# Attention layer 1 in hand-ordered steps: grouping of tiled matmuls, split transposes, value copies on ScalarE, range checks inside the loop

## The chip, the cores and the metric

One core of one Trainium2 chip. The metric is the device time of one execution in microseconds (us); lower is better. Each run is classed as fast or slow by its time and granted clock. A ratio is the mean time of one kernel's fast runs over that of the other's of the same rounds, so not quite the ratio of the medians quoted beside it. "Faster" means by more than 2%.

The engines are called as in the profile: PE (TensorE), PEld (its weight loads), DVE (VectorE), ACT (ScalarE), POOL (GpSimd), SP (SyncE, which issues the DMAs here).

## The reference, cut to what matters

Two layers run over x of 128 x 256 x 256 (rows, positions, channels). Only the second is touched: group norm, then attention within a band of 16 positions, four heads of 64 channels, for each of the 128 rows.

```python
def _L1_conv_ref(x, w_in, b_in, w_out, b_out, band):
    qkv = x2 @ w_in.T + b_in                      # x2: rows x 256 x 256
    q, k, v = jnp.split(qkv, 3, axis=-1)          # four heads of 64 each
    scores = jnp.einsum('bhid,bhjd->bhij', q, k) / jnp.sqrt(D)
    scores = jnp.where(jnp.abs(i - j) <= band, scores, -jnp.inf)
    attn = jax.nn.softmax(scores, axis=-1)
    out = jnp.einsum('bhij,bhjd->bhid', attn, v)
    return out @ w_out.T + b_out
...
x = x + _L1_conv_ref(_gn(x), L1_conv_w_in, ..., 16)
```

Softmax weights of a position sum to 1. A bias of the values therefore comes through attention unchanged, and can be added after it, as `b_v @ w_out.T`.

## The kernel before

Layer 1 handles two rows (a pair) at a time, 64 pairs. A generator prepares the next pair step by step while the present one is scored and applied; the framework's scheduler then fixes the final order on each engine. The names in the profile: `ps_x` transposes, `ps_p` projections of q and k, `ps_v` values, `ps_sc` scores, `ps_o` and `ps_su` the two parts of apply (outputs and sums), `ps_y` the output projection. PE's results lie in banks of PSUM until ACT or DVE have copied them out (an evacuation). `ps_mm` has two PSUM banks, which transposes, projections, values and outputs take in turn. Scores and apply work on tiles of 64 rows (tiled groups); all other groups use the full array of 128 x 128. The lists of the profile show two instructions for each fp32 matmul of the program: a projection of two matmuls is x4.

```python
def prep1(p, d):                                   # next pair, in steps
    xt = sb.tile([P, 2 * NB, C], F32, name="xt1", tag="xt", bufs=3)
    nc.sync.dma_start(xt, rows(x1[s0 // GB], s0 % GB, 2))
    ...
    nc.gpsimd.tensor_tensor(xb, xt, bcast(bout_r, 1, 2 * NB), ALU.add)
    ...
    for k in range(KC):                            # all eight transposes
        ps = mm1("ps_x1")
        for t in range(2 * NB):
            nc.tensor.transpose(ps[...], xt[:, t, k * P : (k + 1) * P], ident)
        nc.scalar.activation(xgT[:, k, :], ps, AF.Identity, bias=nM1[:, k : k + 1])
    yield
    ...                                            # q0 q1 k0 k1, a yield after each
    for r in range(2):                             # values, with their bias on VectorE
        ...
        nc.vector.tensor_tensor(v[:, r, :, :], ps.rearrange(...), bcast(bv1_r, 1, NB), ALU.add)
        yield
...
for p in range(NP):
    for r in range(2):
        es = scores1(d, r)                         # 64x64 tiles, exp, band mask
        next(ahead, None); next(ahead, None)
        late = bool(ends1)
        if todo1: back1()                          # apply (64x32 tiles) and combine
        next(ahead, None)
        if late: end_row1()                        # output projection, sum, store
        next(ahead, None)
        todo1.append((d, r, es))
...
# after the loop: range checks of eb (4096 columns), both sums (2048, 1024), mask (256)
check(eb.rearrange("p h b i -> p (h b i)"), math.exp(-20.0), math.exp(20.0), 0, ck)
...
def check(src, lo, hi, col, pool):
    ...
    nc.vector.tensor_scalar(a, src, lo, None, ALU.is_gt)
    nc.vector.scalar_tensor_tensor(a, src, hi, a, ALU.is_lt, ALU.mult)
    nc.vector.tensor_reduce(ok[:n, col : col + 1], a, AX.X, ALU.min)
```

## Time and profile before

| | before |
|---|---|
| time, median of 4 fast runs | 3526.7 us (3524.7 to 3528.1) |
| first transposes of layer 1 to last output add | 1303.8 us |
| one pair of rows | 20.27 us |
| last output add to end of span | 32.3 us |

The lines behind the table stand in the prediction. How to read them: in a timeline each line is a merged group with its start, duration, engine, source line, operation, names and count. Matmuls overlap in the pipeline, so durations of neighbouring groups overlap too. What a group costs PE is the distance from its start to the start of the next group.

### The profile page before, as it was taken

How to read it: one execution, taken by the hardware profiler on the slowest of the kernel's cores; microseconds unless marked ns; L12 is line 12 of the kernel's file. 1: busy time of each engine (PE TensorE's matmuls, PEld its weight loads, DVE VectorE, ACT ScalarE, POOL GpSimd, SP SyncE). 2: the span in 40 equal slices, each digit the busy share in tenths (PEclk: the TensorE clock that was granted, in tenths of full speed). 3: DMA queues.
4: the chain of work that ended last, by engine and by line, in shares of the span. 5: the costliest groups of instructions: out<-in, count | busy, mean ns of one | idle time of the engine just before them, and what ended most of it. 6: DMA issues, size and time to landing. Idle time of an engine off the chain costs nothing.

```text
span 3522.3 us, 80789 instructions
## 1 busy us (share of the span) xinstructions
PE 3315.2 (94%) x35154; PEld 2034.1 (58%) x35154; DVE 2035.7 (58%) x3284; ACT 1373.5 (39%) x1937; POOL 1975.4 (56%) x1385
## 2 busy tenths in 40 slices
PE   5666999999999999999999996999999999999995
PEld 3333555555555555555555554666666666666664
DVE  5863566666666666666666664444444444444445
ACT  2332444444444444444444442333333333333331
POOL 2356877777777877777777774223323323323331
PEclk8787999999999999999999998999999999999998
DMA  9961122212221222122212221111111111112111
GB/s 285 322 188 45 47 70 70 71 46 70 70 70 46 70 70 71 46 70 70 71 50 76 71 63 60 50 50 62 50 50 62 50 50 62 50 51 61 50 48 48
DMA packets 246812, 263.13 MB, mean 75 GB/s; under 512 B 46000, under 2 KB 212912, under 8 KB 246320
## 3 DMA queue, kind: packets, MB, share of 16 engines
q1 hardware_dynamic: 246448, 257.88, 25.0%
q8 instruction: 278, 4.55, 0.6%
q14 instruction: 86, 0.70, 0.1%
HBM read 189.02 MB, written 68.81 MB: 73 GB/s over the span
## 4 chain that ended last, share of the span: by engine, by line
PE 88%; DMA 3%; ACT 3%; DVE 2%; SPq 2%; POOL 2%; issue 0%; ACTq 0%; DVEq 0%; POOLq 0%
PE ps_p L1233 20%; PE ps_p L1546 14%; PE ps_sc L1267 8%; PE ps_ov L1298 7%; PE ps_v L1560 7%; PE ps_v L1248 6%; PE ps_y L1340 6%; PE ps_y L1630 6%; PE ps_su L1304 3%; PE ps_sc L1585 3%; PE ps_o L1612 3%; DMA zt<-in_z_dram 2%; PE ps_x L1215 2%; ACT e L1593 1%; PE ps_su L1612 1%; ACT xgT L1538 1%
## 5 line engine op out<-in xcount | busy, mean ns | idle before, releaser
L1288 POOL TENSOR_TENSOR eboth<-e 128x512 f32<-128x512 f32 x512 | 640.2, 1271 | 401.4 <-DVE e L1283 401.3
L1283 DVE TENSOR_TENSOR e<-ps_sc,eb 128x1024 f32<-128x1024 f32 x512 | 603.0, 1219 | 338.7 <-ACT ps_sc L1274 249.1
L1274 ACT ACTIVATE ps_sc<-ps_sc 128x1024 f32<-128x1024 f32 x512 | 492.8, 1006 | 507.4 <-PE ps_sc L1267 507.4
L1595 POOL TENSOR_TENSOR e<-e,bw 128x384 f32<-128x384 f32 x256 | 251.2, 1003 | 475.5 <-ACT e L1593 475.5
L1546 PE MATMUL ps_p<-xgT,w_in 128*128 128x512 f32 x1024 | 500.7, 612 | 4.2
L1531 POOL TENSOR_TENSOR xb<-xt,bout_r 128x1024 f32<-128x1024 f32 x64 | 150.7, 2356 | 423.5 <-DVE yo L1634 418.8
L1267 PE MATMUL ps_sc<-qT,kT 32*128 32x256 f32 x4096 | 293.8, 400 | 1.6 <-ACT kT L1237 1.6
L1564 DVE TENSOR_TENSOR v<-ps_v,bv_r 128x512 f32<-128x512 f32 x128 | 84.4, 660 | 362.6 <-PE ps_v L1560 362.6
L1621 DVE TENSOR_TENSOR odd<-ps_o,odd 128x512 f32<-128x512 f32 x128 | 88.5, 692 | 339.9 <-ACT odd L1618 339.8
L1233 PE MATMUL ps_p<-xnT,wq 128*128 128x512 f32 x512 | 255.7, 622 | 20.5 <-POOL xnT L1221 20.5
L1298 PE MATMUL ps_ov<-e,v 128*32 128x256 f32 x4096 | 274.1, 385 | 0.5 <-DVE oT L1312 0.5
L1546 PEld LDWEIGHTS ps_p<-xgT,w_in 128*128 128x128 f32 x1024 | 179.0, 189 | 163.0 <-issue 106.7
L1233 PE MATMUL ps_p<-xgT,wg 128*128 128x512 f32 x512 | 253.9, 618 | 0.0
L1340 PE MATMUL ps_y<-wo,oT 128*128 128x256 f32 x1024 | 243.9, 381 | 7.1 <-POOL oT L1330 7.1
L1560 PE MATMUL ps_v<-w_in,xgT 128*128 128x256 f32 x1024 | 248.3, 385 | 0.0
L1340 PEld LDWEIGHTS ps_y<-wo,oT 128*128 128x128 f32 x1024 | 195.6, 191 | 88.1 <-issue 59.5
L1630 PE MATMUL ps_y<-w_out,oT 128*128 128x256 f32 x1024 | 243.5, 381 | 3.0 <-DVE oT L1623 3.0
L1248 PE MATMUL ps_v<-wv,xnT 128*128 128x256 f32 x1024 | 242.1, 379 | 0.0
L1233 PE MATMUL ps_p<-xnT,wk 128*128 128x512 f32 x512 | 241.9, 595 | 0.0
L1267 PEld LDWEIGHTS ps_sc<-qT,kT 32*128 32x128 f32 x4096 | 185.4, 184 | 94.2 <-issue 70.5
L1630 PEld LDWEIGHTS ps_y<-w_out,oT 128*128 128x128 f32 x1024 | 194.9, 191 | 56.9 <-issue 31.9
L1620 DVE RECIPROCAL rv<-odd 128x256 f32<-128x256 f32 x128 | 224.4, 1753 | 4.3
(159 smaller groups left out, 5090.1 us busy)
## 6 DMA issues: line engine op xcount, KB each, us to landing
xa<-in_x_dram SPq DMA_DIRECT2D x8, 4096.0 KB
xt<-in_x_dram SPq DMA_DIRECT2D x64, 512.0 KB
rvb<-rsum SPq DMA_DIRECT2D x256, 128.0 KB
x<-xo SPq DMA_DIRECT2D x16, 2048.0 KB
xt<-x SPq DMA_DIRECT2D x64, 512.0 KB
out_dram<-yo SPq DMA_DIRECT2D x64, 512.0 KB
rs_r<-rs_d SPq DMA_DIRECT2D x64, 256.0 KB
rs_d<-lrs SPq DMA_DIRECT2D x64, 2.0 KB
```

Source lines behind the costliest of these rows:

```text
L1233: nc.tensor.matmul(ps, w[:, k, m * P : (m + 1) * P], getattr(self, src)[:, k, :], start=(k == 0), stop=(k == KC - 1),)
L1248: nc.tensor.matmul(self.ps_v[:, b * C : (b + 1) * C], self.xnT[:, k, t * P : (t + 1) * P], wv[:, k, :], start=(k == 0), stop=(k == KC - 1),)
L1267: nc.tensor.matmul(self.pss[q // 2][:, q % 2, b, :], self.kT[rs, c, r * I + b * P : r * I + (b + 1) * P], self.qT[rs, c, r * I : (r + 1) * I],
L1274: nc.scalar.activation(self.pss[a], self.pss[a], AF.Exp)
L1283: nc.vector.tensor_tensor(e, pss[a], eb[:, h : h + 2], ALU.mult)
L1288: nc.gpsimd.tensor_tensor(t, es[a][:, :, 0, :], es[a][:, :, 1, :], ALU.add)
L1298: nc.tensor.matmul(ov[q * D0 : (q + 1) * D0, :], self.v[:, r, b, h * D0 : (h + 1) * D0], es[q // 2][:, q % 2, b, :], start=(b == 0), stop= ...
L1340: nc.tensor.matmul(self.ps_y[:, b * C : (b + 1) * C], self.oT[r][:, k, b * P : (b + 1) * P], wo[:, k, :], start=(k == 0), stop=(k == KC - 1),)
L1546: nc.tensor.matmul(ps, w_in[:, k, n * C + m * P : n * C + (m + 1) * P], xgT[:, k, :], start=(k == 0), stop=(k == KC - 1),)
L1560: nc.tensor.matmul(ps[:, b * C : (b + 1) * C], xgT[:, k, t * P : (t + 1) * P], w_in[:, k, 2 * C : 3 * C], start=(k == 0), stop=(k == KC - 1),)
L1595: nc.gpsimd.tensor_tensor(e[:, q], e[:, q], bcast(bw.rearrange("p b w -> p (b w)"), 1, KC), ALU.mult)
L1630: nc.tensor.matmul(ps[:, b * C : (b + 1) * C], oT[:, k, b * P : (b + 1) * P], w_out[:, k, :], start=(k == 0), stop=(k == KC - 1),)
```

## The change

It takes the order of layer 1 out of the scheduler's hands. Scores of one row are followed straight by apply of the row before; the transposes of a pair are split over both steps; values are copied by ScalarE without bias, which moves into the output's bias; and the range checks are cut to 512 columns and run one in an iteration. The output's bias is added to the input in place, after its transposes. In the last pair two value groups are moved between the rest, and each row is stored by itself; the sums of the last eight pairs are checked without a way through memory. In the loop `was`, `now`, `nxt` and `nn` are the pair before, the present one and the next two; `turn` transposes, `combine` adds and divides the parts of apply, `out_row` is output projection, sum and store.

```diff
-    bv1_r = load_row(b_in[2 * C : 3 * C], "bv1_r")
+    bv_c = const.tile([P, KC], F32, name="bv_c")          # four small loads
...
+        for k in range(KC):
+            nc.tensor.matmul(ps[:, :C], bv_w[:, k, :], w_out[:, k, :], ...)
+        nc.vector.tensor_add(bout_r, bout_r, ps[:, :C])   # value bias, through w_out
...
+                self.xt = sb.tile(..., tag="xt", bufs=4)
+            def turn(self, k):                            # four transposes, not eight
+                ...
+                if k == KC - 1:
+                    nc.gpsimd.tensor_tensor(self.xt, self.xt, bcast(bout_r, 1, 2 * NB), ALU.add)
...
-                nc.vector.tensor_tensor(v[:, r, :, :], ps..., bcast(bv1_r, 1, NB), ALU.add)
+                nc.scalar.copy(self.v[:, r, :, :].rearrange("p b c -> p (b c)"), ps)
...
+        with tc.manual_schedule():
+            for p in range(NP - 1):
+                nn = pair1(p + 2)                         # issues the load
+                ...
+                now.scores(0)
+                was.apply(1)
+                was.out_row(0)
+                was.combine(1)
+                nxt.project("qT", 0)
+                nxt.project("kT", 0)
+                nxt.project("qT", 1)
+                nn.turn(0)
+
+                now.scores(1)
+                now.apply(0)
+                now.combine(0)
+                nxt.project("kT", 1)
+                if p < NP - 2:
+                    nxt.values(0)
+                    nxt.values(1)
+                was.out_row(1)
+                nn.turn(1)
+                if checks and p > 0:
+                    checks.pop(0)()
+                was, now, nxt = now, nxt, nn
...                                                       # last pair written out
```

## The prediction

> **What bounds the kernel now.** I read the page first (engine shares, the slices), then busy time by windows, then TensorE's timeline of one pair of rows in layer 1, then VectorE's timeline at the end. Page and windows:
>
> ```profile
> PE 3315.2 (94%) x35154; PEld 2034.1 (58%) x35154; DVE 2035.7 (58%) x3284; ACT 1373.5 (39%) x1937; POOL 1975.4 (56%) x1385
> PE   5666999999999999999999996999999999999995
> 2186.20:3489.30 1303.10, 1295.56 (x19968) 862.02 (x19968) 592.77 (x767) 464.47 (x768) 399.32 (x320) 1.00 0.17 53
> 2351.98:2372.25 20.27, 20.20 (x314) 13.45 (x313) 9.28 (x12) 7.25 (x12) 6.23 (x5) 1.00 0.17 54
> 3490.00:3522.30 32.30, 0.56 (x2) 0.50 (x2) 21.56 (x15) 0.00 (x0) 0.00 (x0) 0.55 0.20 72
> ```
>
> The columns of the windows are PE, weight loads, DVE, ACT, POOL, granted clock, DMA share and GB/s. Layer 1, which is all that changes but for setup, runs from 2186.2 to 3489.3: 64 pairs, one every 20.27 us. PE is busy in 99% of it, at full clock; the next engine, DVE, in 46%. So a change in layer 1 pays only if it shortens PE's own sequence. The last 32.3 us are another stage: PE idle, DVE busy alone. What fills a pair on PE (start, duration, group):
>
> ```profile
> 2351.98 0.93 PE L1612 MATMUL ps_o<-e,v 64*32 64x96 f32 x60
> ...
> 2353.27 1.99 PE L1560 MATMUL ps_v<-w_in,xgT 128*128 128x256 f32 x8
> 2355.11 1.89 PE L1630 MATMUL ps_y<-w_out,oT 128*128 128x256 f32 x8
> 2356.93 0.89 PE L1585 MATMUL ps_sc<-qT,kT 64*64 64x96 f32 x32
> 2357.75 1.15 PE L1537 MATMUL ps_x<-ident,xt 128*128 128x128 f32 x8
> 2358.82 0.51 PE L1612 MATMUL ps_o<-e,v 64*32 64x96 f32 x18
> 2359.41 1.98 PE L1546 MATMUL ps_p<-xgT,w_in 128*128 128x512 f32 x4
> 2361.32 0.73 PE L1612 MATMUL ps_o<-e,v 64*32 64x96 f32 x40
> ...
> 2362.43 1.98 PE L1546 MATMUL ps_p<-xgT,w_in 128*128 128x512 f32 x4
> 2364.25 1.89 PE L1630 MATMUL ps_y<-w_out,oT 128*128 128x256 f32 x8
> 2365.98 1.88 PE L1546 MATMUL ps_p<-xgT,w_in 128*128 128x512 f32 x4
> 2367.79 0.89 PE L1585 MATMUL ps_sc<-qT,kT 64*64 64x96 f32 x32
> 2368.61 1.98 PE L1546 MATMUL ps_p<-xgT,w_in 128*128 128x512 f32 x4
> 2370.43 1.89 PE L1560 MATMUL ps_v<-w_in,xgT 128*128 128x256 f32 x8
> 2372.25 0.93 PE L1612 MATMUL ps_o<-e,v 64*32 64x96 f32 x60
> ```
>
> Read starts, not durations (those overlap). The same four projection instructions take 1.82 from start to next start at 2368.61, which follows a tiled group (64-row tiles); 1.81 at 2365.98, which precedes one; 1.91 at 2359.41, which does both. The y group takes 1.73 at 2364.25, with a full-array group on both sides, and 1.82 at 2355.11, before a tiled one. So going into a tiled stretch costs 0.09 us and coming out 0.10, **about 0.20 us an excursion**, and a projection without either is 1.72. There are five excursions a pair: apply; scores; the first 18 instructions of the other apply; its other 78; scores. That second apply also costs 0.58+1.11 = 1.69 in two pieces, against 1.29 for the whole one.
>
> The end of the run:
>
> ```profile
> 3493.09 2.29 DVE L946 TENSOR_SCALAR chk<-eb 128x4096 f32<-128x4096 f32 x1 [3.06 <-DMA out_dram<-yo]
> 3495.42 4.43 DVE L947 SCALAR_TENSOR_TENSOR chk<-eb,chk 128x4096 f32<-128x4096 f32 x1
> ...
> 3515.58 0.15 DVE L1697 TENSOR_SCALAR verdict<-ok_ps 1x1 int32<-1x1 f32 x1 [0.69 <-PE ok_ps L1696]
> ```
>
> The last output is added at 3490.03, the checks run alone until 3514.7, and the verdict stands at 3515.73, 6.6 us before the end of the span.
>
> **What the Trainium skill says.** "TensorEngine Tiling (Array Packing)", Key Properties: changing the tiling mode drains TensorE. The trace agrees in kind: 0.20 us for each excursion. "Perfetto Trace Analysis", Identifying the Most-Contended Engine: matmul busy time does not tell how close PE is to its limit. It agrees: 20.20 of 20.27 us count as busy with all those switches inside. "TensorE: Matmul & The Clock Gate", Back-to-back issue gap, has 262 cycles for 256 columns and 518 for 512; at the 2.4 GHz named there that is 0.11 and 0.22 us. This trace steps 0.216 and 0.43 in fp32, twice as much, and I use the trace. The same page, The HAM clock gate, has the array at half clock after an idle window; the first transposes of layer 1 step 0.214 us instead of 0.109 after such a pause, so both ends of the loop run partly slow, before and after.
>
> **The change, part by part.**
>
> *PE order.* The instruction order of the changed kernel has per pair: scores, apply, y, three projections, four transposes; then scores, apply, one projection, two values, y, four transposes. Counts of real work stay. Scores and apply now adjoin, so there are two excursions, and apply is never split. Working: 4 projections x 1.72 = 6.88; 4 value and y groups x 1.73 = 6.92; 2 scores x 0.82 = 1.64; 2 applies x 1.29 = 2.58; 8 transposes x 0.109 = 0.87; sum 18.89; 2 x 0.20 = 0.40; **19.29 us a pair**. Checked on the kernel before: the same 18.89 + 5 x 0.20 + 0.40 for the split = 20.29, measured 20.27. That scores followed straight by apply costs no more than 0.82 is seen in the last pair before, at 3471.59 to 3472.41. Gain 0.97 us a pair; one pair's worth is left out for the first and last, so 63 x 0.97 = **61 us**.
>
> *Range checks.* They go into the loop in pieces of 512 columns, by the rows of the old checks about 0.4+0.7+0.7 = 1.8 us of DVE in some 15 of the iterations; DVE is over half idle there. At the end, between the last output add and the verdict, 0.16+0.07+0.56+0.2 = 1.0 us remain, then the 6.6 us: 7.6 in place of 32.3, so **24.7 us** less. The last row's own check (1.1 us at 256 columns) lies in front of the last output add, where DVE had waited 3.4 us for PE.
>
> *Values by ScalarE.* 2 x 0.66 us a pair leave DVE, 2 x 0.59 (the copy of the same shape) come to ACT: 8.4 of 19.3 us there. Off the path: 0. The bias goes through w_out once (two matmuls and an add before the loop): under 1 us.
>
> *Ends.* The final drain keeps its stalls (apply waiting for the combine before it, y waiting for the last combine: 0.3+0.9+1.9 us before), with two value groups moved there to fill some. The first pair is as serial as it was. Net 0, give or take 3.
>
> Sum: 61 + 24.7 = 86 us; 3527.9 - 86 = **3442 us**, -2.4%.
>
> **Rivals.** (a) *The fixed order makes PE wait.* The load of a pair two ahead is now issued at the top of an iteration, after the previous output, and its transposes come after scores, apply, y and three projections: some 8 us later. One load issued at 2340.38 had its last packets at 2343.9, beside an output: 3.5 us. Against it, then; were the load as slow as 9 us, 1 us a pair would come back, 3505 us. The accumulators are the other place: the second apply needs the combine of the first, which on DVE stands behind the y add: 1.83 (y) + 0.25 + 0.68 + 0.41 + 1.75 + 0.69 = 5.6 us after that apply, and PE comes there after 8.3. Slack 2.7 us. (b) *Switches are not what costs*, and each weight change costs the same wherever it is: then only the split of apply (0.40) goes, 25 + 25 = 50 us, 3478. Against: 1.73 and 1.82 for the same y group, by its neighbour alone. (c) *The clock.* PE denser by 5% might be granted less; the loop has 1.00 now. A grant of 0.97 gives back about 37 us: 3479. Nothing speaks for it. (d) *ACT or DVE become the bound*: 8.4 and under 10 of 19.3 us; only their order could hurt, by late release of the two projection banks; each evacuation (0.69 us) has a 1.7 us group beside it.
>
> **Range and chances.** The end stage is nearly sure. The loop is my risk: 0.1 us a pair is 6 us. 0.25 us more than I worked out, from semaphores at the short transposes or an unforeseen wait, would bring 3458, just the 2% line (3457). Fewer switch costs than thought, or a shorter start, could give 10 us more. I take 3428 to 3464. Faster by over 2%: 0.79; within 2%: 0.20; slower: 0.01.
>
> **What would show it.** In the changed profile: a pair every 19.3 us (19.1 to 19.5); scores to apply 0.82 apart with no other group between; no apply in two pieces; projections of 1.72 inside a run of three; no PE wait of over 0.15 us in the loop; checks of 512 columns between the adds and under 9 us from the last output add to the end. A period of 19.8 or more with a wait before the first transposes or before the second apply would make rival (a) right; a period of 19.8 with no waits, rival (b); a granted clock under 0.99 in the loop, (c).

## The result, and the profile after

3439.7 us (median of 4 fast runs, 3437.7 to 3441.4) against 3526.7; ratio 0.9754, 95% interval 0.9737 to 0.9771. Faster by 2.5%; 3442 was predicted.

The windows of the changed kernel: layer 1, one pair, and what follows the last output add. The columns are as in the prediction.

```profile
2186.10:3429.47 1243.37, 1238.83 (x19970) 874.75 (x19970) 598.56 (x714) 545.84 (x896) 407.82 (x320) 1.00 0.19 57
2816.33:2835.60 19.27, 19.27 (x317) 13.66 (x313) 8.11 (x10) 8.53 (x14) 6.24 (x6) 1.00 0.19 56
3429.47:3435.90 6.43, 0.00 (x0) 0.00 (x0) 0.05 (x2) 0.00 (x0) 0.00 (x0) 0.50 0.20 64
```

Layer 1 starts at the same time in both profiles (2186.2 and 2186.1). From there to the last output add it is 60.5 us shorter (1303.83 - 1243.37); from there to the end, 32.3 - 6.5 = 25.8 us. Together 86.3 of the 86.4 us between the spans. PE was busy 99.4% of this stage before and is busy 99.6% of it now, at full clock both times, and the profile notes no wait of PE (over 0.15 us) from 2250 to 3400 us in either kernel: the busy share does not show the gain, the number of pairs per time does. PE's timeline of a pair shows where it lies:

```profile
2814.22 0.89 PE L1605 MATMUL ps_sc<-qT,kT 64*64 64x96 f32 x32
2815.04 0.93 PE L1633 MATMUL ps_o<-e,v 64*32 64x96 f32 x60
...
2816.33 1.99 PE L1664 MATMUL ps_y<-w_out,oT 128*128 128x256 f32 x8
2818.16 5.31 PE L1576 MATMUL ps_p<-xgT,w_in 128*128 128x512 f32 x12
2823.31 0.60 PE L1565 MATMUL ps_x<-ident,xt 128*128 128x128 f32 x4
2823.84 0.89 PE L1605 MATMUL ps_sc<-qT,kT 64*64 64x96 f32 x32
2824.66 0.93 PE L1633 MATMUL ps_o<-e,v 64*32 64x96 f32 x60
...
2825.95 1.98 PE L1576 MATMUL ps_p<-xgT,w_in 128*128 128x512 f32 x4
2827.78 3.62 PE L1591 MATMUL ps_v<-w_in,xgT 128*128 128x256 f32 x16
2831.23 1.89 PE L1664 MATMUL ps_y<-w_out,oT 128*128 128x256 f32 x8
...
2833.49 0.89 PE L1605 MATMUL ps_sc<-qT,kT 64*64 64x96 f32 x32
```

From 2814.22 to 2833.49 is one pair, 19.27 us. There are two stretches of tiled groups (64-row tiles): scores and whole apply, 0.82 + 1.29 us each. The three projections in a row cost 5.15, or 1.72 each. No line carries a wait. The end, on DVE:

```profile
3428.78 0.69 DVE L1668 TENSOR_TENSOR yo<-ps_y,xt 128x512 f32<-128x512 f32 x1 [0.78 <-PE ps_y L1664]
3429.39 0.13 DVE L1760 TENSOR_SCALAR verdict<-ok_ps 1x1 int32<-1x1 f32 x1
```

The verdict follows the last add at once; all that remains is a tail of 6.4 us, which the kernel before has too (6.6).

### The profile page after: what moved, and what is told of

It reads as the page before.

```text
span 3435.9 us, 81082 instructions
## 1 busy us (share of the span) xinstructions
PE 3257.9 (95%) x35158; PEld 2048.2 (60%) x35158; DVE 2019.8 (59%) x3218; ACT 1455.3 (42%) x2065; POOL 1982.7 (58%) x1385
## 5 line engine op out<-in xcount | busy, mean ns | idle before, releaser
L1615 POOL TENSOR_TENSOR e<-e,bw 128x384 f32<-128x384 f32 x256 | 258.9, 1033 | 444.1 <-ACT e L1613 444.1
L1576 PE MATMUL ps_p<-xgT,w_in 128*128 128x512 f32 x1024 | 469.4, 601 | 0.1
L1568 POOL TENSOR_TENSOR xt<-xt,bout_r 128x1024 f32<-128x1024 f32 x64 | 151.9, 2374 | 383.9 <-PE ps_x L1565 383.9
L1668 DVE TENSOR_TENSOR yo<-ps_y,xt 128x512 f32<-128x512 f32 x128 | 88.3, 690 | 379.1 <-PE ps_y L1664 379.1
L1576 PEld LDWEIGHTS ps_p<-xgT,w_in 128*128 128x128 f32 x1024 | 188.9, 190 | 199.8 <-issue 166.6
L1591 PE MATMUL ps_v<-w_in,xgT 128*128 128x256 f32 x1024 | 231.8, 379 | 0.0
L1591 PEld LDWEIGHTS ps_v<-w_in,xgT 128*128 128x128 f32 x1024 | 194.4, 190 | 53.5 <-issue 30.1
L1255 PEld LDWEIGHTS ps_v<-wv,xnT 128*128 128x128 f32 x1024 | 189.6, 190 | 50.9 <-issue 31.1
```

The lines of the kernel that those rows point to most:

```text
L1255: nc.tensor.matmul(self.ps_v[:, b * C : (b + 1) * C], self.xnT[:, k, t * P : (t + 1) * P], wv[:, k, :], start=(k == 0), stop=(k == KC - 1),)
L1576: nc.tensor.matmul(ps, w_in[:, k, n * C + m * P : n * C + (m + 1) * P], self.xgT[:, k, :], start=(k == 0), stop=(k == KC - 1),)
L1591: nc.tensor.matmul(ps[:, b * C : (b + 1) * C], self.xgT[:, k, t * P : (t + 1) * P], w_in[:, k, 2 * C : 3 * C], start=(k == 0), stop=(k == ...
L1615: nc.gpsimd.tensor_tensor(e[:, q], e[:, q], bcast(bw.rearrange("p b w -> p (b w)"), 1, KC), ALU.mult)
```

## The experiments

Theory: in the loop PE waits for nothing, and only its own order counts; each excursion from full-array matmuls to tiled ones and back costs 0.20 us, and cutting apply costs more; the rest of the gain is the bare checks at the end. Rivals: hand order as such (fewer waits), the move of work to other engines, or only the uncut apply.

Start times of layer 1 differ by up to 11 us between runs and chips before anything that was changed. So beside the times I give the length of a pair and the stage from the first transposes of layer 1 to the last output add, both from the traces. That stage was 1243.4 in the changed kernel's own profile, and 1242.1 in two variants with the same loop (e5, e6): differences of 2 us are nothing. Most of that comes from the first projections, during which the granted clock comes back from 0.50 to 1.00, sooner or later: they take 8.95 us to the next group in the changed kernel's profile, 7.99 in e5 and 7.78 in e6, whose start is the same. Without them the three stages agree within 0.4 us.

| kernel | median us (before, same chip) | ratio, 95% interval | pair us | stage us | end us |
|---|---|---|---|---|---|
| before | 3526.7 | | 20.27 | 1303.8 | 32.3 |
| changed | 3439.7 (3526.7) | 0.9754 (0.9737 to 0.9771) | 19.27 | 1243.4 | 6.5 |
| e1, group between | 3469.9 (3531.3) | 0.9824 (0.9807 to 0.9840) | 19.67 | 1266.9 | 6.8 |
| e4, apply cut | 3470.9 (3531.3) | 0.9829 (0.9813 to 0.9845) | 19.73 | 1269.7 | 6.9 |
| e2, old order, late load | 3928.9 (3531.3) | 1.1124 (1.1105 to 1.1142) | 27.29 | 1727.0 | 6.9 |
| e3, the same, cut | 3933.6 (3531.3) | 1.1137 (1.1118 to 1.1156) | 27.30 | 1730.9 | 6.8 |
| e9, old order | 3462.2 (3526.6) | 0.9817 (0.9802 to 0.9832) | 19.62 | 1264.3 | 7.0 |
| e10, old order, cut | 3503.2 (3526.6) | 0.9932 (0.9917 to 0.9947) | 20.27 | 1305.4 | 6.9 |
| e8, transposes together | 3475.3 (3527.0) | 0.9855 (0.9838 to 0.9871) | 19.83 | 1277.8 | 6.5 |
| e5, checks last | 3467.1 (3527.0) | 0.9831 (0.9815 to 0.9847) | 19.27 | 1242.1 | 34.7 |
| e6, no checks | 3439.5 (3527.0) | 0.9753 (0.9737 to 0.9769) | 19.27 | 1242.1 | 6.5 |
| e7, values on VectorE | 3444.1 (3527.0) | 0.9765 (0.9749 to 0.9782) | 19.27 | 1246.4 | 6.9 |
| e11, ends mended | 3439.5 (3526.6) | 0.9753 (0.9740 to 0.9767) | 19.27 | 1241.6 | 6.5 |

All gave correct results.

### e1: one full-array group between scores and apply

```diff
                 now.scores(0)
-                was.apply(1)
                 was.out_row(0)
+                was.apply(1)
...
                 now.scores(1)
-                now.apply(0)
-                now.combine(0)
                 nxt.project("kT", 1)
+                now.apply(0)
+                now.combine(0)
```

> The changed kernel with one full-array group put between scores and apply in both steps (the y group in the first, the fourth projection in the second). Same instructions, two more excursions between tiled and full-array matmuls per pair. Theory (mode switches cost 0.20 us each): a pair takes 19.27 + 2 x 0.197 = 19.66 us, the whole +25 us against the changed kernel, about 3465 us, and the scores are followed by a y group at the same 0.82 us. Rival (what counts is that the order is by hand and apply is whole, not who stands beside whom): 19.27 us, 3440 us.

Measured: 19.67 us a pair, +0.40; the stage 23.5 us longer. PE's timeline:

```profile
2806.69 0.89 PE L1605 MATMUL ps_sc<-qT,kT 64*64 64x96 f32 x32
2807.51 1.98 PE L1576 MATMUL ps_p<-xgT,w_in 128*128 128x512 f32 x4
2809.42 0.93 PE L1633 MATMUL ps_o<-e,v 64*32 64x96 f32 x60
```

The scores still cost 0.82. The projection between two tiled groups costs 1.91, with no wait noted, where it cost 1.82 after apply and 1.72 in a run. Same instructions, same dependencies met; only the neighbours changed. This shows the price of a switch, and refutes the rival that hand order itself, whatever it is, gives the gain. What in the array takes the time is not shown. The trace gives one hint: inside a run of full-array groups the weight load begins a step ahead of its matmul (in the changed kernel at 2827.35 for the value matmul of 2827.78), but after a tiled group it begins with its matmul (both at 2825.95).

### e4: apply cut, and nothing else

```diff
-                was.apply(1)
-                was.out_row(0)
+                was.apply(1, 0, 9)        # its first nine products: 18 instructions
+                was.out_row(0)
+                was.apply(1, 9, 48)
```

> The changed kernel with only the first apply cut after 18 instructions by the y group. Theory: one more excursion and the cut, +0.46 us a pair: 19.73 us, +29 us, about 3469 us. Rival (only the excursion counts, the cut itself is free): +0.20, 19.47 us, +12 us, 3452 us.

Measured: 19.73 us, +0.46, as expected. PE's timeline:

```profile
2814.39 0.52 PE L1637 MATMUL ps_o<-e,v 64*32 64x96 f32 x18
2814.84 1.99 PE L1668 MATMUL ps_y<-w_out,oT 128*128 128x256 f32 x8
2816.76 0.73 PE L1637 MATMUL ps_o<-e,v 64*32 64x96 f32 x40
...
2817.87 5.42 PE L1576 MATMUL ps_p<-xgT,w_in 128*128 128x512 f32 x12
```

The two pieces take 0.45 + 1.11 = 1.56 us in place of 1.29: 0.26 (before rounding) is the cut itself. The excursion is the other 0.20, seen in the y group (1.92 for 1.83) and the projections behind the second piece. How the 0.26 divides between a second end and a second start, no run separates.

### e2 and e3: the old order by hand, with a slip of mine

In these two I moved the eight transposes to the place they had before (right after the first scores), but let them be those of the pair two ahead, whose load is issued at the top of the same iteration.

```diff
                 now.scores(0)
+                nn.turn(0)
+                nn.turn(1)
                 was.apply(1)
-                was.out_row(0)
                 was.combine(1)
                 nxt.project("qT", 0)
+                nxt.project("qT", 1)
+                was.out_row(0)
                 nxt.project("kT", 0)
-                nxt.project("qT", 1)
-                nn.turn(0)

                 now.scores(1)
-                now.apply(0)
-                now.combine(0)
                 nxt.project("kT", 1)
                 ...
                     nxt.values(0)
+                now.apply(0)
+                now.combine(0)
                 ...
                     nxt.values(1)
                 was.out_row(1)
-                nn.turn(1)
```

In e3 the first apply is also cut: `was.apply(1, 0, 9)`, then `nxt.project("qT", 0)`, then `was.apply(1, 9, 48)`.

> The order of groups of the kernel before, laid down by hand in the changed kernel, apply left whole. Theory: four excursions instead of two, in place of 2 x 0.20 some 0.79 us, so 18.89 + 0.8 = 19.7 us a pair, +27 us, about 3466 us. Rival (hand order as such removes waits): near 19.3 us a pair, 3440 us.

> As the run with the old order, with the first apply cut after 18 instructions by a projection, as it stood in the kernel before. Theory: a fifth excursion (0.20) and the cut itself (0.17 for the second end of a tiled group, 0.09 for its second start), +0.46 over that run: about 20.15 us a pair, +55 us over the changed kernel, about 3494 us; the remaining 0.1 to the 20.27 of the kernel before is its projection's wait for the transposed input, which this order does not have. Rival: the cut costs only where it waits, so no more than the run with the old order.

Both missed by far: 27.3 us a pair. SP's timeline of e2 (the issue of a load), then PE's:

```profile
2817.94 0.46 SPq L1557 DMA_DIRECT2D xt<-x  x1
```

```profile
2822.99 1.94 PE L1565 MATMUL ps_x<-ident,xt 128*128 128x128 f32 x8 [5.61 <-DMA xt<-x]
2824.86 1.53 PE L1633 MATMUL ps_o<-e,v 64*32 64x96 f32 x64
```

PE stands for the load in every pair, 5.3 us on average (37 waits, the longest 5.6), and then works at half clock for a while (granted 0.50 from 2822.99 to 2827; eight transposes take 1.87 us to the next group, 1.02 in e9). They tell nothing of the switches, but they are the test that rival (a) of the prediction needed. The load can be used 5.05 us after its issue here, the slowest of 33 (4.6 to 5.05, median 4.8), with an output store of the same size issued 0.5 us ahead of it. The prediction had read 3.5 us off the packets of a load whose store was 2.4 us ahead. In the changed kernel the issue is at 2815.07 and the transposes at 2823.31, 8.24 us later. So the order does hold, with some 3.2 us to spare and not the 4.5 I had counted. A step moved carelessly costs 7.7 us a pair (27.29 against 19.62 in e9), where the whole gain of the loop is 1.00.

### e9 and e10: the old order, its load in time

The same order with `nxt.turn(0)` and `nxt.turn(1)` in place of `nn.turn`, so that a load is a whole pair ahead, as in the kernel before; e9 with apply whole, e10 with it cut where the scheduler had cut it.

```diff
-        for k in range(KC):               # before the loop
-            nxt.turn(k)
...
                 now.scores(0)
-                nn.turn(0)                # against e2; e10: the same against e3
-                nn.turn(1)
+                nxt.turn(0)
+                nxt.turn(1)
```

> The order of the kernel before by hand once more, now faithfully: the transposes are those of the pair projected in the same iteration, so their input was loaded a whole pair earlier. In the first try the transposes came 0.8 us after the issue of their load and TensorE waited 5.6 us for it in every pair, which hid everything else. Apply whole. Theory (0.20 us an excursion): four excursions, 19.7 us a pair, +27 us over the changed kernel, about 3467 us. Rival (hand order as such is the gain): 19.3 us, 3440 us.

> The same with the first apply cut after 18 instructions by the first projection, which is the very order of the kernel before. Theory (the order on TensorE is the whole difference in the loop): the cut and the fifth excursion bring +0.46, the projection's wait for its transposed input some 0.1 more: 20.27 us a pair as before, +63 us over the changed kernel, about 3502 us. Rival (other parts of the change, such as the in-place sum or the values by ScalarE, carry some of the gain): clearly under 20.2 us.

Measured: 19.62 and 20.27 us a pair. PE's timeline of e10:

```profile
2806.55 0.89 PE L1605 MATMUL ps_sc<-qT,kT 64*64 64x96 f32 x32
...
2808.39 0.51 PE L1637 MATMUL ps_o<-e,v 64*32 64x96 f32 x18
2809.03 1.98 PE L1576 MATMUL ps_p<-xgT,w_in 128*128 128x512 f32 x4
2810.94 0.73 PE L1637 MATMUL ps_o<-e,v 64*32 64x96 f32 x40
...
2826.82 0.89 PE L1605 MATMUL ps_sc<-qT,kT 64*64 64x96 f32 x32
```

With the old order of groups the changed kernel has the old length of a pair, to 0.01 us, though values are still on ScalarE, the sum still in place, the checks still inside and the order still by hand. So **the order of the groups on PE is the whole gain of the loop**. From the changed kernel to e9 it is 0.35 for two excursions, not 0.40: with only the eight transposes between scores and apply, the excursion costs 0.15 (1.02 us against 8 x 0.109 = 0.87). From e9 to e10 it is 0.65: 0.20 the excursion, 0.26 the cut (as in e4), and 0.19 that the first piece of apply takes 0.64 us to the next start where 0.45 was its own: the projection behind it waits for the transposed input, which the trace names ACT `xgT`. (From the end of the scores to that projection it is 1.66 us in e10 and in the kernel before alike, though the pieces between divide it differently.) e10 as a whole is 23.4 us under the kernel before by medians: the end of the program, which it kept.

### e8: the transposes together

```diff
                 nn.turn(0)
+                nn.turn(1)
...
                 was.out_row(1)
-                nn.turn(1)
```

> The changed kernel with both groups of transposes at the end of the first step. Theory (two banks): the second group takes the bank of the projection just before the first one, which ScalarE frees about 0.95 us after that projection ends, while the first transposes take 0.44: a wait of 0.5 us a pair, 19.8 us, +31 us, about 3471 us. Rival (the split does not matter; number of excursions is the same): 19.27 us, 3440 us.

Measured: 19.83 us, +0.56; the stage +34.4. PE's timeline:

```profile
2822.14 0.60 PE L1565 MATMUL ps_x<-ident,xt 128*128 128x128 f32 x4
2823.08 0.66 PE L1565 MATMUL ps_x<-ident,xt 128*128 128x128 f32 x4 [0.34 <-ACT qT L1580]
```

The second four start 0.94 us after the first, where 0.44 is their work: they want the bank of the projection just before the first four, and `qT` is the evacuation of that bank. Four transposes are too short to cover an evacuation of 0.69 us; with a long group behind each of them, as in the split, nothing waits. So in this order the transposes are better split, though that saves no switch.

### e5 and e6: the checks after the loop, and no checks

```diff
-                if checks and p > 0:
-                    checks.pop(0)()
...
+        while checks:                     # e5; e6 drops them
+            checks.pop(0)()
         tot = sm.tile([P, 1], F32, name="okmin", bufs=1)
```

> The changed kernel with its fifteen range checks of 512 columns (1.8 us each on VectorE by the changed kernel's trace: 0.42 + 0.69 + 0.69) put after the loop. Theory: they lie bare at the end, 15 x 1.8 = +27 us, about 3467 us, and the pair stays at 19.27 us. Rival (the checks in the loop cost something there, so taking them out gives part back): less than +20 us and a shorter pair.

> The changed kernel without the fifteen checks (those of the last pairs stay), so not a kernel to use. Theory: VectorE has the time, so nothing changes in the loop: 3440 us, within 2 us. Rival: VectorE's checks hold up an evacuation now and then, and the time falls by up to 15 x 0.5 = 7 us.

e5: +27.4 us by medians, all in the end (34.7 against 6.5), the pair unchanged. Its window after the last add shows DVE busy alone:

```profile
3430.53:3465.20 34.67, 0.56 (x2) 0.50 (x2) 25.88 (x47) 0.00 (x0) 0.00 (x0) 0.50 0.03 10
```

e6 (which omits part of the guard, so is no kernel to use) is as long as the changed kernel: 3439.5 against 3439.7. Inside the loop the checks cost nothing that can be measured.

### e7: the values on VectorE, with their bias

```diff
-                nc.scalar.copy(self.v[:, r, :, :].rearrange("p b c -> p (b c)"), ps)
+                nc.vector.tensor_tensor(self.v[:, r, :, :], ps..., bcast(bv1_r, 1, NB), ALU.add)
```

The bias of the values is then no longer put into that of the output.

> The changed kernel with the values written by VectorE with their bias, as before, and the bias no longer in the output's. Theory: off the path; VectorE is done with the combine about 4.0 us after apply ends and frees the first value bank at about 4.7, TensorE wants it at 5.3: no change, 3440 us within 3, 19.27 us a pair. Rival (VectorE was a second bound, moving the values off it was needed): a wait before the y group of up to 0.5 us a pair, +30 us.

Measured: 19.27 us a pair, nothing in the loop. The stage is 3.0 us longer than the changed kernel's and 4.3 longer than that of e6 (3.8 to 3.9 for both without the first projections), in the last pair alone: there the value addition stands on DVE behind the combine and the check of the row before, and the next value group waits 1.9 us for its bank; the granted clock after that is 0.66 (3418 to 3423), where it is 1.00 in the changed kernel (3417 to 3423). So the move to ScalarE was not needed in the loop; it helps a little where the loop drains.

### e11: the two ends mended

Eight unused matmuls in the pause before the first load lands, so that the clock is up; in the last pair, apply of its first row ahead of the second value group.

```diff
+        warm = mm1("ps_warm")
+        for i in range(8):
+            nc.tensor.matmul(warm[:, :C], bv_w[:, i % KC, :], w_out[:, i % KC, :], ...)
...
             now.values(0)
-            was.out_row(0)
             now.scores(1)
-            now.values(1)
+            was.out_row(0)
             now.apply(0)
             now.combine(0)
+            now.values(1)
             was.out_row(1)
             now.apply(1)
```

> The changed kernel with its two ends mended: eight unused matmuls (of the output weights by the bias) while TensorE waits for the first load of layer 1, so that the clock is up when the work starts, and in the last pair the first apply right after the y group, so that the second finds the combine done. The loop is left: 19.27 us. Theory: the first projections take 6.9 to 7.5 us instead of 8.95 and the transposes 1.1 instead of 2.0 (-2 to -3 us), the wait of 1.6 us before the last apply goes; together -3 to -5 us, about 3436 us, near the noise, so the trace's stages decide. Rival: the start is paced by the evacuations and the load, not the clock, and only 1.5 us go.

Measured: 3439.5 us in 5 runs, no difference from the changed kernel; the stage 1241.6, within the 2 us that mean nothing. PE's timeline of the start tells why the first half gave less than I had hoped:

```profile
2189.25 1.35 PE L1568 MATMUL ps_x<-ident,xt 128*128 128x128 f32 x8 [3.31 <-DMA xt<-x]
2190.78 8.37 PE L1579 MATMUL ps_p<-xgT,w_in 128*128 128x512 f32 x16 [0.18 <-ACT xgT L1569]
```

The warming matmuls and the setup transposes ended at 2185.9 and the load let PE go on at 2189.25. The transposes began at the fast step (0.109 us), but fell to 0.213 at the eighth, and the first projections stepped 0.854 before they came back to 0.429: the granted clock was 1.00 in the pause of 3.3 us and 0.53 from 2189.9 to 2193.5. That the pause is what cost the clock is likely and not tested. Besides, the 8.95 us that I had expected to shorten were a long case (7.78 in e6); here it is 8.20. In the last pair the wait of the last apply for the combine before it shrank from 1.4 to 0.8 us, but that combine ended later: from the end of the apply before to the start of the last one it is 4.71 us, and 3.42 in the changed kernel. No version here beats the changed kernel by more than the noise.

## Why the prediction was right

- **Switches, 0.20 us an excursion, five made two: right.** e1 adds two and costs 0.40; e9 and e10 walk the whole way back. It is not one price for all: with transposes alone between two tiled groups it was 0.15 (e9).
- **The cut apply, 0.40 us: right as a sum, not as one thing.** 0.26 is the cut (e4). The rest was a wait of the projection behind the first piece for its transposed input, 0.14 in the kernel before and 0.19 in e10. The prediction charged it all to the cut; it goes with the cut, so the sum held.
- **19.29 us a pair: measured 19.27.** The loop's 61 us: measured 60.5, and that this agrees so well is partly luck. 64 pairs at 1.00 would be 64. The first projections, at a slower clock for longer, gave 1.4 us back (8.95 us to the next group against 7.60), most of which is chance and no cost of the change: the same start takes 7.69 us in e2 and 9.14 in e3. The other 2 us lie at the end: from the 120th of the 128 output adds to the last, four pairs, it is 57.7 us before and 56.0 now, 1.7 less and not 4. The prediction left one pair's gain out for both ends together, and took the gain of a pair as 0.97, where its own figures give 0.98.
- **The end, 24.7 us: measured 25.8.** I had 1.0 us of minimum, product and verdict after the last add. They do not depend on that add, and ran beside the last output.
- **Values on ScalarE, 0: right in the loop (e7)**, but not in the last pair, where the working had not looked: about 4 us.
- **Rival (a), a wait by the fixed order: did not happen** (no wait of PE is noted in the loop, before the transposes or before the second apply), but the slack of the load was overstated (5.05 us for the load, not 3.5), and e2 shows the rival was real. **The split of the transposes** the prediction counted only as the same eight instructions. e8 shows that without it 0.56 us of each pair would have gone to a PSUM bank. Here the prediction was right with a reason missing.
- **Rival (b)** (only the cut counts) falls by e1; **(c)**: the clock granted in the loop stayed at 1.00; **(d)**: DVE and ACT were busy 8.1 and 8.5 of 19.3 us, and taking the checks away (e6) changed nothing.

What stays open: how the 0.40 us that two excursions still cost in a pair could be avoided (no order was tried that has one excursion a pair), and what the array does in that time.

## What to carry to other kernels

On an engine that is busy all the time, look at start-to-start distances of equal groups with different neighbours: the difference is the price of the order, and it is in no busy share. Put the tiled matmuls of different kinds next to each other: scores followed by apply cost the same 0.82 us here as scores followed by a full-array group. Keep each group whole, and put a long group after each short one that takes a PSUM bank. When a loop is ordered by hand, check each load's issue against its first use in the new order, and put work that is independent of the end into an engine's idle time inside the loop.

## What the Trainium skill lacked or had wrong

- "TensorEngine Tiling (Array Packing)", Key Properties, says that changing the mode drains TensorE, with no size. Here: 0.09 us going into 64-row tiles and 0.10 coming out, 0.40 for two excursions (e1); a tiled group that is cut costs 0.26 more than its excursion (e4). From tiles of 64 x 64 to 64 x 32 (scores, then apply) no cost is seen: 0.82 and 1.29 us, with either neighbour.
- "TensorE: Matmul & The Clock Gate", Back-to-back issue gap, gives cycles that are 0.11 and 0.22 us for 256 and 512 columns at 2.4 GHz. The section's table names no data type. The fp32 instructions of these loops step 0.216 and 0.429 us at full granted clock, and each fp32 matmul of the program is two of them.
- "TensorE: Matmul & The Clock Gate", PE-mode transpose, says that the full clock does not engage for transposes. Between matmuls they step 0.109 us here, half of the 0.214 after a pause, so they do run at a clock that others have raised; whether transposes alone raise it, no run shows.
- No page that I read gives the time from issue to use of a load beside a store. Here: 4.6 to 5.05 us for 512 KB in pieces of 1 KB, with a store of 512 KB issued 0.5 us ahead (e2).
